# Image 0 of an attention layer: eight transposed runs in 96 steps for seven in 100, and the last group's column sums added on Pool

## The chip, the cores and the metric

The kernel runs on one core of a Trainium2 chip. The core has five engines that run at the same time and wait for each other by semaphores: PE (TensorE, matrix products), ACT (ScalarE, functions of one element, exp above all), DVE (VectorE), POOL (GpSimd) and SP (which here only issues DMAs). The trace lists PE's weight loads apart, as PEld. The metric is the device time of one execution in microseconds (us), as the median of several runs.

## The reference

The input is `x`, 4 images of 64 x 64 positions with 64 channels, float32. Four layers follow one another:

- layer 0: attention over the 4096 positions of an image, with query, key and value projections, times `gamma`, plus `x`
- layer 1: layer norm, a 1x1 convolution to 256 channels, a 3x3 depthwise convolution, a gate (product of the two halves), a scale by the channel means, a 1x1 convolution back, residual; then norm, 1x1, gate, 1x1, residual
- layer 2: attention of the image with itself, without weights
- layer 3: attention with projections to 32 channels, then a batch norm over all images, residual

The change lies in layer 2 of image 0:

```
def _L2_conv_ref(x):
    B, C, H, W = x.shape
    xf = x.reshape(B, C, H * W)
    scores = jnp.einsum('bci,bcj->bij', xf, xf)
    attn = jax.nn.softmax(scores, axis=-1)
    return jnp.einsum('bcj,bij->bci', xf, attn).reshape(x.shape) + x
```

`scores` is symmetric, 4096 x 4096 for each image: what is true of the pair (i, j) is true of (j, i).

## The kernel before

**Order of work.** The program is a list of items, one per step of an attention layer, that `run` (L1843) emits in order: layer 0 of images 0 to 3 (32 items each), layer 2 of image 0 (100 items), then layer 2 of image b and layer 3 of image b - 1 in turn. Each engine executes its own instructions in the order in which they are emitted. Beside the items run two lanes (`Lane`, L995): `conv` holds setup and layer 1, `misc` the projections, the features of layer 2 and the like. A lane is a generator that emits a piece of work and yields a price in microseconds; each item "ticks" the lane by some amount, and the lane emits its next piece when the ticks have paid for it. Layer 1 of image b starts two items after layer 0 of image b has ended, so layer 1 of image 3 runs beside layer 2 of image 0 and its tail beside layer 2 of image 1.

**Layer 2** (`layer2`, L1324). The 4096 columns and rows are cut into 8 groups of 512. A block (h, g) is exp(scores) for the columns of group h and the rows of group g. It takes two steps (u = 0, 1) of 256 rows. A step (`item`, L1495) does this:

- `score` (L1377): four matmuls (L1390, eight records in the trace) into a PSUM slot of 1024 columns, one of three that all work takes in turn; two exps on ACT (L1395) write half of an `e` tile and add up the rows. An `e` tile holds the two steps of a pair; the pool has six tiles, shared with `xr` (image 0's transposed weights), `esum` and `own`.
- `products` (L1445), two or three items later: four matmuls (L1451) add e times x into the accumulator of group h. When group h ends, ACT copies the accumulators to an `own` tile (L1463; image 0 only) and DVE adds that to `m.A` (L1466).

**Transposed runs.** Where the lists have a pair, such as `(1, 2)` in group 0, the blocks (0, 1) and (0, 2) also serve as (1, 0) and (2, 0), which are then not computed. For each of a pair's four steps DVE transposes e (`turned`, L1408), and a run of 64 matmuls (`turned_products`, L1468; L1477; 128 records) multiplies the transposed tiles with `xr`; DVE reads its two slots into `m.A` (L1490 or L1492). Image 0 issues a run three items after its last step, as long as an item of its layer 2 is left. The row sums of the mirrored blocks are column sums of e: `column_sums` (L1412). For image 0 Pool issues a DMA for each step (L1424) that copies or adds e to one of two halves of `esum`, and one at the group's end that adds the halves (L1428), and then adds the remaining two quarters (L1432); for the other images Pool itself adds e to `esum` (L1430, L1432). `spread_sums` (L1434), nine items after a group's last mirrored step, transposes and reduces `esum` on DVE; if the layer has ended by then, it comes at the sixth item of the next layer.

Image 0 uses the lists `PART`, images 1 to 3 `FULL` (L1317). Which groups of image 0 have pairs: 0, 1, 6 and 5, in this order of time; the order of groups is 0, 1, 2, 3, 4, 7, 6, 5.

**What stands around it.** In an item of image 0 the lane `conv` is ticked by 3.3, but by 1.5 in the seven items around the last step of the third run (`slow`, items 20 to 26), and `misc` by 1.8. Layer 1 of image 3 (L1199) uses them so: norm (L1159), whose factors SP spreads by DMA (L1183) and DVE multiplies in (L1191); 1x1 matmuls (L1205); two halves (r = 1, then r = 0) of 4 x 9 depthwise multiply-adds on DVE (L1240, L1243, L1251), each half beginning with ACT's writes to `pad` (L1222); `ytot`, the sum over positions (L1257); `sca`, the product for the scale (L1260); 1x1 (L1269); the second norm (L1170 to L1191); four pieces of 1x1, gate and 1x1 (L1205, L1290, L1294, L1297). From item 89 on, `features2(1)` (L1302) transposes image 1 on PE (L1309), in four pieces that DVE and then ACT copy (L1312) and SP spreads by DMA (L1313). `close2(0)` (L1529) scales and adds image 0's result in items 10, 13, 22, 32 and 42 of image 1; it first reduces the row sums, in one instruction for each run of groups with equal counts (L1540).

Of the kernel before, what the change touches and what calls it, by code (L numbers as in the profile page):

```python
# [691 lines left out]
def fast_path(ctx: ExitStack, tc: tile.TileContext, a: dict, out: bass.AP, bad):  # L692
# [43 lines left out]
    def piece():  # L736
        if turn_of["banks"]:
            return PS[:, bass.ts(new_bank(), 512)]
        return new_ps()[:, 0:512]
# [8 lines left out]
    def new_e(name="e"):  # L748
        return ep.tile([128, 2048], F32, tag="e", name=name)
# [4 lines left out]
    def new_big(name):  # L754
        return big.tile([128, 4096], F32, tag="big", name=name)
# [236 lines left out]
    def at(i, fn):  # L992
        due.setdefault(i, []).append(fn)
# [308 lines left out]
    def features2(b):  # L1302
        x = X[:, b]
        im[b].ko = ko = new_big("ko")
        kv = ko[:, 0:N].rearrange("p (a e n) -> p a e n", e=2, n=128)
        for g in range(4):
            ps = piece()
            for i in range(4):
                nc.tensor.transpose(ps[:, bass.ts(i, 128)], x[:, bass.ts(4 * g + i, 128)], ident)  # L1309
            for e, copy in enumerate((nc.vector.tensor_copy, nc.scalar.copy)):  # L1310
                own, other = slice(64 * e, 64 * e + 64), slice(64 - 64 * e, 128 - 64 * e)
                copy(kv[own, bass.ts(g, 4), e, :], ps[own, :].rearrange("p (a n) -> p a n", n=128))  # L1312
                nc.sync.dma_start(out=kv[other, bass.ts(g, 4), e, :], in_=kv[own, bass.ts(g, 4), e, :])  # L1313
            yield 3.0
# [1 line left out]
    SIDES = [[(7, (h + 1) % 7), ((h + 2) % 7, (h + 3) % 7)] for h in range(7)]  # L1316
    FULL = [(7, [7])] + [(h, [h] + SIDES[h]) for h in range(6)] + [(6, SIDES[6] + [6])]  # L1317
    PART = [
        (0, [0, 7, (1, 2), 5, (3, 4), 6]), (1, [1, 2, (5, 6), 3, 4, 7]), (2, [2, 1, 3, 4, 7]),
        (3, [3, 1, 2, 4, 7]), (4, [4, 1, 2, 3, 7]), (7, [7, 0, 1, 2, 3, 4]),  # L1320
        (6, [6, (2, 3), 0, (4, 7), 5]), (5, [5, (2, 3), 0, (4, 7), 6]),
    ]

    def layer2(b, when_free=None):  # L1324
# [87 lines left out]
        def column_sums(n):  # L1412
            h, _, _, run, _ = steps[n]
            if run is None:
                return
            k, e = mine_t[h].index(n), st["e"][n]
            if k == (0 if b == 0 else 1):
                st["esum"][h] = new_e("esum")
            if h not in st["esum"]:
                return  # L1420
            esum = st["esum"][h][:, 0:1024]
            if b == 0:
                both = st["esum"][h]
                nc.gpsimd.dma_start(  # L1424
                    out=both[:, bass.ts(k % 2, 1024)], in_=e, **({} if k < 2 else {"accum_op": ALU.add})
                )
                if n == mine_t[h][-1]:
                    nc.gpsimd.dma_start(out=esum, in_=both[:, 1024:2048], accum_op=ALU.add)  # L1428
            else:
                nc.gpsimd.tensor_add(esum, st["e"][mine_t[h][0]] if k == 1 else esum, e)  # L1430
            if n == mine_t[h][-1]:
                nc.gpsimd.tensor_add(esum[:, 0:512], esum[:, 0:512], esum[:, 512:1024])  # L1432
# [96 lines left out]
    def close2(b):  # L1529
        x, m = X[:, b], im[b]  # L1530
        ps, tot, n = piece(), sums2[:, b, :], 4 * max(m.mirrored) + 4
        cs = m.cs.rearrange("p (j k) -> p j k", k=4)
        for k in range(4):
            mm(ps[32 * k : 32 * k + 32, 0:n], sel4, cs[:, 0:n, k], start=True, stop=True)
        g = 0
        while g < 8:
            k = g
            while k < 8 and m.count[k] == m.count[g]:
                k += 1
            nc.vector.tensor_reduce(  # L1540
                tot[:, 4 * g : 4 * k],
                m.zs[:, m.first[g] : m.first[g] + 4 * m.count[g] * (k - g)]
                .rearrange("p (t k) -> p t k", k=m.count[g]), AX.X, ALU.add,
            )
            g = k
        nc.vector.tensor_add(tot[:, 0:n], ps[:, 0:n], tot[:, 0:n])
        rz = sm.tile([128, 32], F32, tag="rz2", name="rz2")
        nc.vector.reciprocal(rz, tot)
        yield
        for i in range(4):  # L1550
            ps = new_ps()
            for j in range(8):
                c = 1024 * i + 128 * j
                nc.tensor.transpose(ps[:, bass.ts(j, 128)], m.A[:, c : c + 128], ident)
            blocks_ = ps.rearrange("p (j n) -> p j n", n=128)
            nc.vector.tensor_mul(
                blocks_, blocks_, rz[:, bass.ts(i, 8)].unsqueeze(2).to_broadcast([128, 8, 128])
            )
            xs = x[:, bass.ts(i, 512)].rearrange("p (j h) -> p j h", h=H)
            for o in range(2):  # L1560
                nc.vector.tensor_add(xs, ps.rearrange("p (j o h) -> p j o h", j=8, o=2)[:, :, o, :], xs)  # L1561
            yield
# [9 lines left out]
    def open3(b):  # L1572
        x, m = X[:, b], im[b]
        m.tg = new_big("tg")
        m.th = m.tg[:, 0:1024]
        m.gx = m.tg[:, 1024:2048].rearrange("p (t d) -> p t d", d=32)
        for nb in range(2):
            ps = piece()
            for jj in range(2):
                for s in range(2):  # L1580
                    k = 2 * s + jj
                    mm(
                        ps[32 * k : 32 * k + 32, :], thw[64 * s : 64 * s + 64, :],
                        tok(x, s, 2 * nb + jj), start=True, stop=True,
                    )
            nc.vector.tensor_scalar_add(m.th[:, bass.ts(nb, 512)], ps, V("L3_conv_theta_b"))
            yield 3.0

        m.own = own = m.tg[:, 2048:3072].rearrange("p (s n) -> p s n", s=2)
        for s in range(2):  # L1590
            ps = piece()
            for j in range(4):
                mm(
                    ps[32 * j : 32 * j + 32, :], phw[64 * s : 64 * s + 64, :],
                    tok(x, s, j), start=True, stop=True,
                )
            nc.vector.tensor_scalar_add(own[:, s, :], ps, V("L3_conv_phi_b"))
            yield 3.0
        for i in range(2):
            ps = piece()  # L1600
            for t in range(8):
                mm(ps[:, bass.ts(t, 64)], x[:, bass.ts(8 * i + t, 128)], gw, start=True, stop=True)
            for s in range(2):
                nc.vector.tensor_add(
                    m.gx[:, 16 * s + 8 * i : 16 * s + 8 * i + 8, :],
                    ps.rearrange("p (t s d) -> p t s d", s=2, d=32)[:, :, s, :],
                    gb.unsqueeze(1).to_broadcast([128, 8, 32]),
                )
            yield 3.0

    def keys3(b):
        m = im[b]
        m.ph = new_big("ph")
        keys = m.ph.rearrange("p (s n) -> p s n", s=2)
        for j in range(4):
            for k in range(4):
                nc.sync.dma_start(
                    out=keys[32 * k : 32 * k + 32, :, bass.ts(j, 512)],
                    in_=m.own[32 * j : 32 * j + 32, :, :],
                )  # L1620
# [185 lines left out]
    conv_from, misc_from, misc_to = {}, {}, {}  # L1806
# [9 lines left out]
    for b in range(B):  # L1816
        misc_to[len(items)] = True
        f = len(items)
        if b == 0:
            layer2(b)  # L1820
            misc_from[f + 89] = [features2(b + 1)]
        else:
            layer2(b, lambda b=b: keys3(b - 1))
            turns = close2(b - 1)
            for i in (10, 13, 22, 32, 42) if b == 1 else (8, 12, 22, 32, 42):
                at(f + i, lambda turns=turns: next(turns))
            misc_from[f + 46] = [open3(b - 1)]
            f = len(items)
            misc_to[f] = True
            layer3(b - 1)  # L1830
            if b + 1 < B:
                turns = features2(b + 1)
                for i in (4, 7, 10, 13):
                    between3[f + i] = 2, lambda turns=turns: next(turns)
    f = len(items)
# [174 lines left out]
@with_exitstack  # L2010
def conv_seq_kernel(ctx: ExitStack, tc: tile.TileContext, a: dict, out: bass.AP):
    nc = tc.nc
    flag = ctx.enter_context(tc.tile_pool(name="flag", bufs=1))
    bad = flag.tile([1, 1], mybir.dt.int32, name="bad")
    fast_path(tc, a, out, bad)
    n_bad = nc.values_load(bad[0:1, 0:1], min_val=0, max_val=1 << 20)
    with tc.If(n_bad > 0):
        general_path(tc, a, out)
# [37 lines left out]
```

## Time and profile before

| | us |
|---|---|
| median of 3 runs | 2454.41 (2452.31 to 2454.88) |
| the profiled execution | 2454.17 |
| its span | 2452.4 |
| layer 2 of image 0, from the first product to the last | 1033 to 1249 |
| PE busy in that stretch of 216 us | 209.2 |
| ACT, DVE, Pool busy in it | 151.2, 155.3, 28.9 |
| mean share of the DMA engines in it | 0.47 |

Granted clock: 1.00 in all of these stretches. In the lists of instructions a line gives the start, the length, the engine, the source line, the operation, what it writes and reads, the shape and the number of records; in brackets the idle time of the engine before it and what ended that. Matmuls are pipelined: lengths overlap, and the time between two starts is what one costs. Waits on PE are found by these brackets; the page's share of busy time is a mean over stages with different limits.

### The profile page before, as it was taken

What the parts mean: (1) busy time and instruction counts of PE and PEld (TensorE: products, weight loads), DVE (VectorE), ACT (ScalarE), POOL (GpSimd) and SP (SyncE); (2) the same over time, 40 slices, a digit from 0 to 9 for tenths busy, and PEclk for the clock granted to TensorE, in tenths of its full rate; (3) what the DMA queues carried; (4) which work ended last, traced back from release to release, by engine and by line L of the source; (5) the groups of instructions that cost most, each with busy time, mean ns of one, the idle gap of its engine ahead of it and who ended that gap; (6) DMA issues with size and microseconds to landing.
All of it is one profiled execution on the core that took longest, in us unless ns stands there. A gap on an engine that the chain in (4) does not pass through costs nothing.

```text
span 2452.4 us, 63404 instructions
## 1 busy us (share of the span) xinstructions
PE 2412.2 (98%) x27381; PEld 930.4 (38%) x27381; DVE 1466.6 (60%) x1784; ACT 1651.8 (67%) x3146; POOL 531.7 (22%) x383
## 2 busy tenths in 40 slices
PE   9999999999999999999999999999999999999998
PEld 3343453336433643345334442144421344421113
DVE  2010377227722773378656668876668866678886
ACT  4666766666666676668664459954489744579996
POOL 2000000000000000010135561256631355622110
PEclk9999999999999999999999999999999999999999
DMA  3000000000000000150630026610075300386554
GB/s 80 1 18 1 19 1 18 18 19 1 18 18 11 8 18 18 48 127 2 136 72 20 20 66 134 140 25 24 15 155 117 74 21 20 74 168 142 118 118 116
DMA packets 67668, 136.39 MB, mean 56 GB/s; under 512 B 13004, under 2 KB 34229, under 8 KB 67381
## 3 DMA queue, kind: packets, MB, share of 16 engines
q0 software_dynamic: 24320, 86.55, 17.5%
q1 hardware_dynamic: 42309, 43.85, 7.8%
q8 instruction: 217, 3.56, 0.6%
q10 hardware_dynamic: 752, 1.85, 0.2%
q14 instruction: 70, 0.57, 0.1%
HBM read 4.80 MB, written 4.19 MB: 4 GB/s over the span
## 4 chain that ended last, share of the span: by engine, by line
PE 85%; DVE 9%; ACT 4%; issue 1%; SPq 1%; DMA 0%; DVEq 0%; ACTq 0%
PE PS L1121 18%; PE PS L1095 18%; PE PS L1390 9%; PE PS L1451 9%; PE PS L1639 8%; PE PS L1700 8%; PE PS L1477 7%; DVE tg L1691 3%; PE PS L1205 2%; ACT e L1650 2%; DVE y L1240 2%; DVE X L1561 1%; ACT e L1100 1%; PE PS L1170 1%; PE PS L1063 1%
## 5 line engine op out<-in xcount | busy, mean ns | idle before, releaser
L1100 ACT ACTIVATE e<-PS 128x1024 f32<-128x1024 f32 x512 | 524.2, 1024 | 332.2 <-PE PS L1095 299.6
L1395 ACT ACTIVATE e<-PS 128x512 f32<-128x512 f32 x632 | 371.5, 596 | 334.2 <-PE PS L1390 313.5
L1121 PE MATMUL PS<-e,vq 64*64 64x512 f32 x4096 | 577.1, 592 | 0.0
L1095 PE MATMUL PS<-X,q 64*64 64x512 f32 x4096 | 575.0, 591 | 1.8 <-DVE X L979 1.7
L1650 ACT ACTIVATE e<-PS 128x512 f32<-128x512 f32 (+2 forms) x588 | 500.2, 920 | 59.3 <-PE PS L1639 37.9
L1691 DVE TENSOR_TENSOR tg<-tg,e 128x2048 f32<-128x2048 f32 x172 | 393.8, 2290 | 42.8 <-ACT e L1650 30.8
L1390 PE MATMUL PS<-ko 64*64 64x512 f32 x2528 | 342.8, 596 | 1.1 <-ACT e L1395 0.6
L1451 PE MATMUL PS<-e,X 64*64 64x512 f32 x2528 | 335.6, 590 | 0.9 <-DVE X L1133 0.6
L1240 DVE SCALAR_TENSOR_TENSOR y<-pad,vec,y 128x1024 f32<-128x1024 f32 x240 | 309.1, 1288 | 15.9 <-ACT y L1236 8.5
L1430 POOL TENSOR_TENSOR esum<-esum,e 128x1024 f32<-128x1024 f32 x126 | 299.2, 2375 | 53.6 <-ACT e L1395 46.7
L1408 DVE STREAM_TRANSPOSE turned<-e 128x1024 f32<-128x1024 f32 x196 | 240.6, 1237 | 104.4 <-ACT e L1395 104.4
L1639 PE MATMUL PS<-tg,ph 32*64 32x512 f32 x4096 | 295.5, 612 | 1.7 <-ACT e L1650 0.8
L1095 PEld LDWEIGHTS PS<-X,q 64*64 64x64 f32 x4096 | 184.0, 133 | 258.9 <-issue 179.4
L1121 PEld LDWEIGHTS PS<-e,vq 64*64 64x64 f32 x4096 | 184.1, 133 | 252.0 <-issue 156.0
L1424 POOL DMA_DIRECT2D esum<-e x28 | 22.0, 787 | 1170.7 <-ACT e L1395 1158.9
L1700 PE MATMUL PS<-e,tg 128*32 128x512 f32 x2048 | 272.5, 604 | 0.0
L1108 DVE TENSOR_REDUCE sums<-zs 128x1 f32<-128x4 f32 x128 | 19.6, 153 | 260.4 <-ACT e L1100 260.2
L1451 PEld LDWEIGHTS PS<-e,X 64*64 64x64 f32 x2528 | 104.9, 133 | 168.1 <-issue 144.9
L1672 POOL DMA_DIRECT2D xn<-e x116 | 101.3, 906 | 292.4 <-ACT e L1650 205.0
L1390 PEld LDWEIGHTS PS<-ko 64*64 64x64 f32 x2528 | 97.9, 132 | 163.4 <-issue 136.6
L1639 PEld LDWEIGHTS PS<-tg,ph 32*64 32x64 f32 x4096 | 63.4, 129 | 223.4 <-ACT e L1650 191.0
L1395 ACT ACTIVATION_READ_ACCUMULATOR e<-PS 128x1 f32 x632 | 127.4, 202 | 0.0
(218 smaller groups left out, 1712.9 us busy)
## 6 DMA issues: line engine op xcount, KB each, us to landing
xn<-e POOLq DMA_DIRECT2D x132, 512.0 KB, 5.3
esum<-e POOLq DMA_DIRECT2D x28, 512.0 KB, 5.2
xn<-t SPq DMA_DIRECT2D x64, 128.0 KB
ph<-tg SPq DMA_DIRECT2D x64, 128.0 KB
xn<-X SPq DMA_DIRECT2D x224, 32.0 KB
xr<-X SPq DMA_DIRECT2D x176, 32.0 KB
ko<-ko SPq DMA_DIRECT2D x32, 128.0 KB
xr<-in_x_dram SPq DMA_DIRECT2D x13, 256.0 KB
```

The costliest lines, as they stand in the source:

```text
L1095: mm(ps[64 * c : 64 * c + 64, bass.ts(r, 512)], m.q[rows_, 128 * t + 64 * c : 128 * t + 64 * c + 64], x[rows_, bass.ts(g, 512)], start=Tru ...
L1100: act(es[g // 2][:, bass.ts(g % 2, 1024)], ps, AF.Exp, bias=SHIFT0, accum_out=zs[:, g : g + 1],)
L1121: ins = mm(PS[64 * s : 64 * s + 64, 2048 + 512 * j : 2560 + 512 * j], vq[rows_, :], es[j // 2][rows_, k : k + 512], start=t == 0 and i < 2 ...
L1240: stt(y1, win, wt, y1, ALU.mult, ALU.add)
L1390: mm(ps[64 * c : 64 * c + 64, bass.ts(r, 512)], m.ko[rows_, k : k + 64], m.ko[rows_, bass.ts(h, 512)], start=True, stop=True,)
L1395: act(e[:, bass.ts(r, 512)], ps[:, bass.ts(r, 512)], AF.Exp, bias=SHIFT2, accum_out=slot(g, 2 * u + r),)
L1430: nc.gpsimd.tensor_add(esum, st["e"][mine_t[h][0]] if k == 1 else esum, e)
L1451: mm(st["acc"][r][64 * c : 64 * c + 64, :], xw[rows_, 4 * g + 2 * u + c, :], st["e"][n][rows_, bass.ts(c, 512)], start=n == mine[h][0], st ...
L1639: mm(PS[64 * c : 64 * c + 64, bass.ts(banks[k], 512)], m.ph[32 * k : 32 * k + 32, 128 * mc + 64 * c : 128 * mc + 64 * c + 64], m.th[32 * k ...
L1650: act(e[:, 512 * lo : 512 * k], PS[:, 512 * banks[lo] : 512 * banks[lo] + 512 * (k - lo)], AF.Exp,)
L1691: nc.vector.tensor_add(esum, esum, e)
L1700: mm(st["y"][32 * k : 32 * k + 32, :], m.gx[:, i % 32, :], es[i][:, bass.ts(k, 512)], start=mc == 0, stop=i % 32 == 31,)
```

## The change

Three edits. The lists of image 0 are cut anew. Group 0 loses the direct block 5 and group 6 the direct block 5; group 5 has `(0, 6)` as a third pair where it had the direct blocks 0 and 6, and that pair stands for the two blocks that went. Together 96 steps for 100, and eight pairs for seven; the pairs of groups 6 and 5 now follow one another without direct steps between. `slow` is worked out from the third run and moves to items 18 to 24.

The column sums of group 5 in image 0 no longer go by DMA: Pool adds them, as it does for the other images, from the group's second mirrored step on.

The features of image 1 start at item 86 for 89.

```diff
     PART = [
-        (0, [0, 7, (1, 2), 5, (3, 4), 6]), (1, [1, 2, (5, 6), 3, 4, 7]), (2, [2, 1, 3, 4, 7]),
+        (0, [0, 7, (1, 2), 6, (3, 4)]), (1, [1, 2, (5, 6), 3, 4, 7]), (2, [2, 1, 3, 4, 7]),
         (3, [3, 1, 2, 4, 7]), (4, [4, 1, 2, 3, 7]), (7, [7, 0, 1, 2, 3, 4]),
-        (6, [6, (2, 3), 0, (4, 7), 5]), (5, [5, (2, 3), 0, (4, 7), 6]),
+        (6, [6, 0, (2, 3), (4, 7)]), (5, [5, (2, 3), (4, 7), (0, 6)]),
     ]
...
             k, e = mine_t[h].index(n), st["e"][n]
-            if k == (0 if b == 0 else 1):
+            moved = b == 0 and h != 5
+            if k == (0 if moved else 1):
                 st["esum"][h] = new_e("esum")
             if h not in st["esum"]:
                 return
             esum = st["esum"][h][:, 0:1024]
-            if b == 0:
+            if moved:
                 both = st["esum"][h]
                 nc.gpsimd.dma_start(
                     out=both[:, bass.ts(k % 2, 1024)], in_=e, **({} if k < 2 else {"accum_op": ALU.add})
                 )
...
         if b == 0:
             layer2(b)
-            misc_from[f + 89] = [features2(b + 1)]
+            misc_from[f + 86] = [features2(b + 1)]
```

## The prediction

> **What bounds the kernel now.** I read the page's totals and its chain first, then TensorE's order of time in layer 2 of image 0 (about 1033 to 1249 us), then who keeps TensorE waiting there.
>
> ```profile
> PE 2412.2 (98%) x27381; PEld 930.4 (38%) x27381; DVE 1466.6 (60%) x1784; ACT 1651.8 (67%) x3146; POOL 531.7 (22%) x383
> PE 85%; DVE 9%; ACT 4%; issue 1%; SPq 1%; DMA 0%; DVEq 0%; ACTq 0%
> ```
>
> TensorE is busy nearly all the span, and the chain lies on it for 85%. So TensorE work that goes is time that goes, unless TensorE then waits longer. The price of that work, from the order of time on PE (start, length):
>
> ```profile
> 1329.42 1.04 PE L1390 MATMUL PS<-ko 64*64 64x512 f32 x8
> 1330.28 1.04 PE L1451 MATMUL PS<-e,X 64*64 64x512 f32 x8
> 1331.25 3.71 PE L1477 MATMUL PS<-turned,xr 32*64 32x256 f32 x128
> 1334.89 1.09 PE L1390 MATMUL PS<-ko 64*64 64x512 f32 x8
> 1335.80 1.04 PE L1451 MATMUL PS<-e,X 64*64 64x512 f32 x8
> ```
>
> Neighbours overlap, so read from start to start. A score (L1390) takes 0.86 us, a product (L1451) 0.86: 1.72 a step. A turned run (L1477, 128 records) takes 3.64, and the groups beside it start 0.11 and 0.05 later than usual: 3.80.
>
> The waits that the change touches, on PE and then on DVE:
>
> ```profile
> 1181.34 0.35 PE L1260 MATMUL PS<-ytot,sca 128*128 128x1 f32 x2 [0.96 <-DVE ytot L1257]
> 1222.69 1.09 PE L1390 MATMUL PS<-ko 64*64 64x512 f32 x8 [0.15 <-ACT ko L1312]
> 1226.44 0.66 PE L1309 MATMUL PS<-ident,X 128*128 128x128 f32 x4 [0.94 <-ACT ko L1312]
> 1241.11 1.09 PE L1205 MATMUL PS<-xn,pw 64*64 64x512 f32 x8 [2.04 <-DVE xn L1191]
> 1280.64 1.09 PE L1205 MATMUL PS<-xn,pw 64*64 64x512 f32 x8 [0.66 <-DVE A L1492]
> ```
>
> ```profile
> 1181.03 0.16 DVE L1257 TENSOR_REDUCE ytot<-ysum 128x1 f32<-128x8 f32 x1
> 1181.11 0.68 DVE L1466 TENSOR_TENSOR A<-own,A 128x512 f32<-128x512 f32 x1
> 1238.70 1.25 DVE L1408 STREAM_TRANSPOSE turned<-e 128x1024 f32<-128x1024 f32 x1 [0.91 <-ACT e L1395]
> 1239.87 1.18 DVE L1191 TENSOR_TENSOR xn<-xn,X 128x1024 f32<-128x1024 f32 x1
> 1275.15 2.35 DVE L1297 TENSOR_TENSOR X<-X,t 128x512 f32<-128x512 f32 x1 [0.18 <-ACT t L1295]
> ```
>
> These PE waits come to 4.75 us. The last line is an add whose median is 0.69 us; it ran beside four Pool adds in a row (1269.71 to 1279.74).
>
> **The change part by part.** Items are numbered from the start of image 0's layer 2.
>
> *The lists.* 100 steps become 96: minus 4 x 1.72 = 6.88 us of TensorE. There are eight runs for seven, but a run is issued three items after its last step, and in both lists the last run ends too late for that (97 of 0 to 99; 95 of 0 to 95). The trace agrees: 6144 records of L1477 are 48 runs, 6 of image 0 and 42 of the others. So seven are issued for six: plus 3.80. Sum on TensorE: -3.08.
>
> Off the path: ACT loses 4 x 2 x (0.60 + 0.20) = 6.4 us; DVE gains four transposes (1.24 each) and four reads of a run (0.42 each), 6.6 us. From 1181 to 1249 ACT is busy 39.6 and DVE 36.6 of 68 us, and TensorE has that stretch covered; without that cover the 6.6 us would show whole. Close2 has six reduces for five: +0.18 us (L1540 rows) ahead of a scale that TensorE's next turned run can wait on.
>
> *Column sums of group 5.* Eight Pool DMA issues of 0.86 and the closing one go (nine transfers of 512 KB, landing after some 5.2); eleven adds of 2.37 come: 11 x 2.37 + 1.27 = 27.3 us on Pool. Cover: the twelve steps hold 12 x 1.72 plus three turned runs of 3.80 and four feature groups of 0.6, some 34 us of TensorE. Pool keeps up, and is ready for the first add at step 85: group 6's last add ended 12.7 us after its last DMA issue (1205.17 to 1217.89), and steps 82 to 85 with their run and convolution work take about as long. Spread_sums for group 5 comes five items into image 1, over 8 us after the last exp, against 3.7 for two Pool instructions. Queued behind Pool's adds is nothing until image 1's first sums. Cost 0; if the cover is gone, see the slower rival.
>
> *Group ends, two or four items earlier against image 3's layer 1.* The convolution lane is paid 3.3 an item, so its work keeps its item number up to 95, while groups 1 to 7 now end two items earlier. Group 7's add into A (L1466, 0.68) stood right behind ytot on DVE; its products end at item 69 now, so it stands ahead: ytot 0.6 later. From 1131.35 to 1181 DVE runs without a gap, so this reaches TensorE whole. Earlier, the slow stretch of the lane (items 20 to 26, now 18 to 24) leaves three more multiply-adds of 1.30 after the third run, and group 2's two adds (1.41) come before the half's end, against two more steps of time (3.44): +1.9, of which 1.07 is slack (1123.86 to the pad write at 1124.93). ACT's pad write, and with it the start of DVE's second half, is up to 0.8 later. I take 0.5, between 0 (ACT catches up) and 0.9. Together the 0.96 wait grows by 1.1 (0.6 to 1.5).
>
> *Multiply by the norm (L1191).* Its first half stays at item 95, now the last of the layer; its matmul follows in the next item, as before. It stands behind a transpose that waits for the exp. TensorE's work in between grows by two products, with which the layer closes (1.72), so the wait of 2.04 would fall to 0.3. But Pool now adds beside it, and two operands in SBUF cost L1297 1.66 us more. Three quarters of the time an add is running: I take +1.0, between 0 and 1.7. New wait 1.3, a gain of 0.7 (1.7 to 0).
>
> [...]
>
> *Features of image 1, items 86 to 90 (were 89 to 93).* Its eight SP transfers of 128 KB no longer run beside Pool's; SP's loads of xr keep their items (0, 10, 40, 50), at least 14 ahead of their runs. Each ACT copy stands behind a DVE copy, behind a transpose; all four meet a transpose (three before), but the adds from group 6's own copy are over earlier. Wait 1.1 before; I take 1.1, bounds 0 and 2.2.
>
> *Tail of image 3's layer 1.* It ends at item 18 of image 1, was 14. The wait of 0.66 recurs (item 10 has a matmul of L1205 in both), and two more pieces fall between runs: +0.2 with the reduce, bounds -0.3 and +1.0. Behind it the program is the same, and shifts.
>
> Sum: -3.08 + 1.1 - 0.7 + 0 + 0.2 = -2.5 us. The profiled execution took 2454.17 us (span 2452.4 and 1.8 around it), 0.24 under the median of 2454.41; so 2451.7 in a run like it, 2451.9 as a median. Bounds of the terms: -3.08 + 0.6 - 1.7 - 1.1 - 0.3 = -5.6, and -3.08 + 1.5 + 0 + 1.1 + 1.0 = +0.5.
>
> **Rivals.**
>
> *The waits go too.* If ytot is no later (ACT and DVE have slack I don't see), and the L1191 and feature waits vanish with the DMA traffic (busy share 0.73 to 0.94 in most of 1180 to 1250): -3.08 - 2.04 - 1.09 = -6.2, 2448.2. Against it: none of these waits is put down to a DMA.
>
> *The order is worse, the work less.* The tail in image 1, the feature copies and the e buffers (two sums held through items 18 to 22 and 85 to 90, of six) each cost their upper bound and one more exp wait of about 2 us: +0.5 + 2, 2456.9. For it: TensorE waited 1.81 for an exp at 1047. Against it: the layer has only some 7 us of PE waits in all.
>
> *Slower: group 6's transfers hold up Pool.* They are eight in a row now. At 9.6 us (the longest landing) for 5.2, four in a chain, the last lands 17.6 us later; Pool's adds may start about 9 late before pairs are held and TensorE waits: 17.6 - 9 - 3.1, +5.5, 2459.9. It decides from a lateness over 9 us. Against it: the median is 5.2 with the same neighbours.
>
> *The change saves nothing*, if TensorE waits for DVE anyway: 0, 2454.4. DVE was gapless only up to 1181; the removed steps lie after it.
>
> **How the numbers follow.** 0.2% is 4.9 us, about what a measurement can tell from no change. Forecast 0.54; waits go too 0.21; order worse 0.12; slower 0.08; nothing saved 0.05. Faster: the second case (0.20 of it) and a little of the first, 0.22. Slower: the fourth and a third of the third, 0.12. Same: 0.66. The forecast's own range is 2448.8 to 2454.9. Wanted are 8 in 10: from the second case to just short of the slower one, 2448.0 to 2457.0.
>
> **What would show it.** Right: 896 records of L1477 in image 0; 96 steps; 11 adds of 2.37 in group 5 with Pool idle between; L1260 waiting about 2 us; L1191 longer than 1.18 or its wait under 2; image 1 shifted by 2 to 3 us with the rest unchanged. Wrong: a wait on Pool ahead of L1395 or L1390, exps waiting for e buffers, a PE wait over 3 us in items 74 to 95, or a changed image 1 after item 20.

## The result: 0.13% slower

The changed kernel takes 2457.61 us (median; 2456.23 to 2462.32), the kernel before 2454.57 beside it. The ratio is 1.0013, with a 95% interval of 1.0007 to 1.0019. The forecast was 2451.9 with a range up to 2457.0: the time lies above the range. The changed kernel's profiled execution took 2457.62 us; its span of 2455.5 is 3.1 longer than the one before.

The totals and the chain of the changed kernel's page:

```profile
PE 2410.4 (98%) x27445; PEld 918.3 (37%) x27445; DVE 1473.2 (60%) x1793; ACT 1645.6 (67%) x3130; POOL 551.5 (22%) x385
PE 83%; DVE 9%; ACT 4%; issue 1%; DMA 1%; SPq 1%; POOL 0%; DVEq 0%; ACTq 0%; POOLq 0%
```

TensorE has 64 records more than before, as worked out (four steps of 16 less, one run of 128 more), and is busy 1.8 us less. The work shrank and the span grew, so TensorE waits longer. POOL and POOLq are new in the chain. Who keeps TensorE waiting in layer 2 of image 0 (line, releaser, its line: us in all, times, longest):

```profile
PE PS L1390 <- DVE A L1493: 5.5, 2, 5.2
PE PS L1205 <- DVE xn L1191: 1.5, 1, 1.5
PE PS L1205 <- ACT e L1395: 1.2, 1, 1.2
PE PS L1309 <- ACT ko L1312: 0.9, 1, 0.9
PE PS L1478 <- ACT ko L1312: 0.9, 1, 0.9
...
PE PS L1260 <- DVE ytot L1257: 0.4, 1, 0.4
```

The first line has no counterpart before. L1493 is DVE's copy of a transposed run from PSUM (lines from 1418 on have moved by one). Here it is in DVE's order of time, around the third run, which ended on TensorE at 1086.2:

```profile
1081.62 0.71 DVE L1441 STREAM_TRANSPOSE esum<-esum 128x512 f32<-128x512 f32 x1
1091.95 0.69 DVE L1442 TENSOR_REDUCE cs<-esum 128x16 f32<-128x512 f32 x1 [9.63 <-POOL cs L1439]
1092.56 1.41 DVE L1493 COPY A<-PS 128x256 f32<-128x256 f32 x4
```

In the kernel before the same reduction waits for nobody:

```profile
1085.09 0.69 DVE L1441 TENSOR_REDUCE cs<-esum 128x16 f32<-128x512 f32 x1
```

In the changed kernel DVE stands still for 9.63 us at the reduction of group 0's column sums, because Pool has not yet zeroed `cs`, the tile that it writes. Pool's order of time says why:

```profile
1080.38 0.90 POOL L1425 DMA_DIRECT2D esum<-e  x1 [2.51 <-DMA esum<-e]
1085.57 0.87 POOL L1429 DMA_DIRECT2D esum<-esum  x1 [4.29 <-DMA esum<-e]
1090.51 1.25 POOL L1433 TENSOR_TENSOR esum<-esum 128x512 f32<-128x512 f32 x1 [4.08 <-DMA esum<-esum]
1091.72 0.19 POOL L1439 MEMSET cs<- 128x128 f32 x1
```

The same in the kernel before:

```profile
1082.39 0.88 POOL L1424 DMA_DIRECT2D esum<-e  x1 [2.27 <-ACT e L1395]
1082.96 0.53 POOL L1438 MEMSET cs<- 128x128 f32 x1
1084.16 0.88 POOL L1424 DMA_DIRECT2D esum<-e  x1 [0.68 <-ACT e L1395]
1090.23 0.86 POOL L1428 DMA_DIRECT2D esum<-esum  x1 [5.18 <-DMA esum<-e]
1095.27 1.27 POOL L1432 TENSOR_TENSOR esum<-esum 128x512 f32<-128x512 f32 x1 [4.18 <-DMA esum<-esum]
```

The memset of 0.19 us stands in `spread_sums(0)`, which comes at item 22 in both kernels (group 0's last mirrored step is item 13 in both). Group 1's mirrored steps, however, moved from items 20 to 23 up to items 18 to 21. So the memset was emitted among group 1's four transfers before, and is emitted behind the whole group now: behind the closing transfer, which waits until the four have landed, and behind the closing add, which waits until the closing transfer has landed. Behind DVE's reduction stand the PSUM reads of the third run; until they are done TensorE has no slot to score into:

```profile
1087.09 1.04 PE L1452 MATMUL PS<-e,X 64*64 64x512 f32 x8
1093.36 1.98 PE L1390 MATMUL PS<-ko 64*64 64x512 f32 x8 [5.23 <-DVE A L1493]
1095.12 1.93 PE L1452 MATMUL PS<-e,X 64*64 64x512 f32 x8
1096.82 1.93 PE L1390 MATMUL PS<-ko 64*64 64x512 f32 x8
1098.53 1.26 PE L1452 MATMUL PS<-e,X 64*64 64x512 f32 x8
```

After the wait of 5.23 us the groups stand 1.76, 1.70, 1.71 and 1.09 apart, not 0.86 to 0.91: 2.77 us more. The windows show the reason (busy us of each engine, then the granted clock, PEclk, then the DMA share and GB/s):

```profile
1080.00:1088.00 8.00, 8.00 (x172) 4.00 (x162) 2.33 (x4) 4.23 (x12) 1.76 (x2) 1.00 0.70 136
1088.00:1093.40 5.40, 0.17 (x8) 0.05 (x4) 1.45 (x4) 0.58 (x3) 1.40 (x2) 0.89 0.54 114
1093.40:1096.00 2.60, 2.60 (x16) 0.77 (x20) 2.56 (x4) 0.56 (x2) 0.00 (x0) 0.50 0.20 51
1096.00:1099.00 3.00, 3.00 (x20) 0.94 (x16) 2.93 (x3) 0.90 (x5) 0.00 (x0) 0.50 0.13 33
1099.00:1102.00 3.00, 3.00 (x32) 1.00 (x28) 2.89 (x4) 2.31 (x8) 0.00 (x0) 1.00 0.02 5
```

The clock is halved for some 6.8 us (5.6 in two windows, 1.2 in the window at 0.89). The wait and the half clock together cost 5.23 + 2.77 = 8.0 us.

The account nearly closes. From the first exp of layer 2 (1019.49 before, 1018.50 after) to one and the same exp of image 1 (the read of its row sum, at 1401.12; 1404.64) the changed kernel takes 386.14 us for 381.63: +4.51. Of that -3.08 is TensorE's work, +8.0 this stall, and the other listed waits are 0.7 shorter (8.0 for 8.7), which makes +4.2; 0.3 us are left over. Ahead of it that execution was 0.99 shorter and behind it 0.4, where the change alters nothing: 4.51 - 0.99 - 0.4 = 3.1, the difference of the spans.

### The profile page after: what moved, and what is told of

Same layout as the page of the kernel before. It is cut to its first block, busy times and chain, and to the rows that moved or that the text cites. A ratio compares the mean times of both kernels' runs of the same rounds, so it can differ in the third digit from the quotient of the medians.

```text
span 2455.5 us, 63512 instructions
## 1 busy us (share of the span) xinstructions
PE 2410.4 (98%) x27445; PEld 918.3 (37%) x27445; DVE 1473.2 (60%) x1793; ACT 1645.6 (67%) x3130; POOL 551.5 (22%) x385
## 4 chain that ended last, share of the span: by engine, by line
PE 83%; DVE 9%; ACT 4%; issue 1%; DMA 1%; SPq 1%; POOL 0%; DVEq 0%; ACTq 0%; POOLq 0%
PE PS L1121 18%; PE PS L1095 18%; PE PS L1390 8%; PE PS L1640 8%; PE PS L1452 8%; PE PS L1701 8%; PE PS L1478 7%; DVE tg L1692 3%; PE PS L1205 2%; DVE y L1240 2%; ACT e L1651 2%; ACT e L1395 1%; DVE turned L1408 1%; DVE X L1562 1%; ACT e L1100 1%
## 5 line engine op out<-in xcount | busy, mean ns | idle before, releaser
L1395 ACT ACTIVATE e<-PS 128x512 f32<-128x512 f32 x624 | 366.2, 595 | 342.3 <-PE PS L1390 319.8
L1390 PE MATMUL PS<-ko 64*64 64x512 f32 x2496 | 336.1, 599 | 6.2 <-DVE A L1493 5.5
L1431 POOL TENSOR_TENSOR esum<-esum,e 128x1024 f32<-128x1024 f32 x136 | 323.2, 2377 | 59.5 <-ACT e L1395 52.0
L1452 PE MATMUL PS<-e,X 64*64 64x512 f32 x2496 | 327.5, 592 | 1.4 <-ACT own L1464 0.8
L1408 DVE STREAM_TRANSPOSE turned<-e 128x1024 f32<-128x1024 f32 x200 | 245.8, 1238 | 107.0 <-ACT e L1395 107.0
L1425 POOL DMA_DIRECT2D esum<-e x20 | 15.6, 782 | 1151.5 <-ACT e L1395 1031.1
L1452 PEld LDWEIGHTS PS<-e,X 64*64 64x64 f32 x2496 | 97.8, 133 | 172.9 <-issue 152.5
L1390 PEld LDWEIGHTS PS<-ko 64*64 64x64 f32 x2496 | 89.9, 133 | 173.7 <-issue 143.8
```

Source lines behind the costliest of these rows:

```text
L1390: mm(ps[64 * c : 64 * c + 64, bass.ts(r, 512)], m.ko[rows_, k : k + 64], m.ko[rows_, bass.ts(h, 512)], start=True, stop=True,)
L1395: act(e[:, bass.ts(r, 512)], ps[:, bass.ts(r, 512)], AF.Exp, bias=SHIFT2, accum_out=slot(g, 2 * u + r),)
L1452: mm(st["acc"][r][64 * c : 64 * c + 64, :], xw[rows_, 4 * g + 2 * u + c, :], st["e"][n][rows_, bass.ts(c, 512)], start=n == mine[h][0], st ...
```

## The experiments

Kernels with added lines have their numbers shifted by up to three: L1390, L1442 and L1478 of the changed kernel are L1393, L1444 and L1480 in most.

**Theory and rivals.** W: the memset's place in Pool's queue costs some 8 us, and the rest of the change gains what was forecast. Rivals: D, that it is DVE's wait as such, with the multiply-adds that it delays, which costs; and that the new lists are worse in themselves.

**cs_zeroed_early**: the changed kernel, with `cs` zeroed at the first score of the layer.

```diff
+                if b == 0:
+                    m.cs = sm.tile([128, 128], F32, tag="cs2", name="cs2", bufs=1)
+                    nc.gpsimd.memset(m.cs, 0.0)
...
-                m.cs = sm.tile([128, 128], F32, tag="cs2", name="cs2", bufs=1)
-                if b == 0:
-                    nc.gpsimd.memset(m.cs, 0.0)
+                if b:
+                    m.cs = sm.tile([128, 128], F32, tag="cs2", name="cs2", bufs=1)
```

> The changed kernel, but the zeroing of cs (a Pool memset of 0.19 us) is emitted at item 0 of image 0's layer 2, not at item 22, where in the changed kernel it stands on Pool behind the closing transfer and the closing add of group 1. Theory W (the wait): this memset holds DVE for 9.6 us, DVE's reads of the third run hold TensorE for 5.2, and TensorE's clock at 0.50 afterwards costs 2.8 more. All 8.0 go: about 2449.6 us (2448 to 2451.5), under the kernel before, with no DVE wait on POOL and clock 1.00 from 1088 to 1100. Rival D (DVE is late anyway: the moved slow stretch and group ends put more on DVE there): the wait moves to ytot, under 3 us gained, 2454.5 to 2456.5. Rival P (Pool's eleven adds or the closer runs cost the time): as the changed kernel, 2457.6 within 1.

Measured: 2451.83 us (2450.02 to 2455.80), ratio to before 0.9993 [0.9984, 1.0002]. DVE's order of time now:

```profile
1083.07 0.69 DVE L1444 TENSOR_REDUCE cs<-esum 128x16 f32<-128x512 f32 x1
1087.18 1.42 DVE L1495 COPY A<-PS 128x256 f32<-128x256 f32 x4 [3.42 <-PE PS L1480]
```

The reduction waits for nobody, the PSUM reads wait for the run alone, TensorE has no wait there, and the clock is 1.00 from 1080 to 1106. That is 5.8 us off the median (4.9 by the ratios, since the two kernels were measured in different rounds) and 7.35 off the stretch between the two exps (378.79). The difference between these numbers lies at least in part at item 10, whose wait varies between executions, of which more below. The median is 0.3 above the range expected of this run. It is 2.35 us under the kernel before beside it (2454.18), with an interval that just includes no change. That it meets the forecast's 2451.9 to 0.1 us is partly luck: seven executions lie at 2450.0 to 2452.0 and four at 2454.7 to 2455.8.

**before_spread_late**: the kernel before, with the memset moved behind group 1's closing add by coming two items later.

```diff
-        spread_at = {mine_t[h][-1] + (5 if b else 9): h for h in m.mirrored}
+        spread_at = {mine_t[h][-1] + (5 if b else 11 if h == 0 else 9): h for h in m.mirrored}
```

> The kernel before, with one edit: the spreading of group 0's sums, and the memset in it, moves from item 22 to item 24, so that the memset stands behind group 1's closing transfer and add, as in the changed kernel. The lists, the DMA sums and the features are untouched. Theory W: DVE waits until about 1097 for the memset, TensorE for some 5 us behind the third run, then half clock: 5 to 9 us more, 2460 to 2463.5. Rivals D and P, to which the lists or Pool's adds matter: 0 to 2 us more.

Measured: 2461.35 us (2459.94 to 2463.31), ratio 1.0031 [1.0019, 1.0043]: the stall can be made in the kernel before, without one step of the change. Its memset stands at 1094.90, right behind the closing add (1093.69). DVE, and TensorE:

```profile
1095.13 0.69 DVE L1441 TENSOR_REDUCE cs<-esum 128x16 f32<-128x512 f32 x1 [8.90 <-POOL cs L1438]
```

```profile
1097.73 1.98 PE L1390 MATMUL PS<-ko 64*64 64x512 f32 x8 [5.90 <-DVE A L1492]
```

**before_spread_late_cs_early** is its control: the same late sums, with `cs` zeroed early by the edit shown above.

> Control of the run before it in this list: the kernel before, spreading of group 0 at item 24 as there, but the memset at item 0. Theory W: the place of the spreading itself costs nothing, as the kernel before within 1 us (2453.6 to 2455.6). If moving DVE's two instructions by two items were what costs, it would be as slow as the run before it.

Measured: 2454.14 us, ratio 1.0004 [0.9995, 1.0013]. Two items more or less for the sums themselves are free; the two kernels differ in the memset's place alone, and are 7.2 us apart.

**cs_zeroed_between**: the changed kernel, with the memset between group 1's closing transfer and its closing add.

```diff
                     nc.gpsimd.dma_start(out=esum, in_=both[:, 1024:2048], accum_op=ALU.add)
+                    if h == 1:
+                        m.cs = sm.tile([128, 128], F32, tag="cs2", name="cs2", bufs=1)
+                        nc.gpsimd.memset(m.cs, 0.0)
```

> The changed kernel, but the memset stands on Pool between group 1's closing transfer and its closing add: DVE still waits for it, but until about 1086.7 and not 1091.9, before the third run has ended (1086.2) by little. Theory W: what costs is TensorE's wait and the clock after it, not DVE's; DVE's wait of some 4 us stays and the time is within 1 us of the run with the memset at item 0, 2449.5 to 2451.5. Rival D (each microsecond DVE loses here is paid at ytot): about 4 us slower than that run, 2453 to 2455.

Measured: 2452.67 us (2450.15 to 2455.79), ratio 0.9992 [0.9983, 1.0001]. DVE still waits here, and TensorE does not:

```profile
1091.08 0.69 DVE L1444 TENSOR_REDUCE cs<-esum 128x16 f32<-128x512 f32 x1 [3.98 <-POOL cs L1432]
```

A wait of 3.98 us on DVE costs nothing, one of 9.63 costs 8: it counts from where the third run's reads become due. The median is over the range that was expected (2449.5 to 2451.5) and close to D's 2453, so it doesn't decide; the trace does. TensorE has no wait at the third run, and its wait for `ytot`, where D would be paid, is 1.03 us, for 1.02 in cs_zeroed_early. What makes the profiled execution long is a wait at item 10 (below). D falls.

With the cause found, four kernels went after the rest of the change, each with `cs` zeroed early and one edit more. They are compared with cs_zeroed_early, which was measured in an earlier round (the kernel before took 2454.18 us beside it, 2453.75 beside these four). Each ratio is known to some 2.2 us, so differences of medians of 1 to 2 us are not clear of noise by themselves; the stretch between the two exps and the waits in the profiles carry these readings, one execution each.

**cs_early_dma_sums** (`moved = b == 0`): group 5's sums by DMA again.

> cs_zeroed_early with the column sums of group 5 back on the DMAs, as before the change. By my theory (the changed kernel lost its time to the memset alone; Pool's adds cost TensorE about nothing, because the multiply L1191, stretched from 1.18 to 2.41 us beside an add, has the last two products of the layer ahead of its matmul): the multiply is back at about 1.18, the wait of L1205 on it goes from 1.5 to between 0.3 and 2, and the time stays within 1.5 us of cs_zeroed_early's 2451.8. Rival (Pool's adds hold DVE up and this is paid by TensorE): the wait falls by the whole 1.2 us and the time to about 2450.5. Rival (the transfers collide with the features of image 1): the wait of L1309 grows from 0.9 to 2 or more, time 2453 or above.

Measured: 2455.56 us (2453.04 to 2458.27), ratio 1.0005 [0.9996, 1.0014]. The third expectation has the time and the collision, but the wrong place: L1309 still waits 0.94. The multiply L1191 is back at 1.18 us and TensorE's wait for it is gone, but the first score of image 1 waits for its features:

```profile
1251.45 1.09 PE L1393 MATMUL PS<-ko 64*64 64x512 f32 x8 [2.33 <-DMA ko<-ko]
```

From the last run to the common exp the profiled execution takes 2.24 us more than cs_zeroed_early: 2.33 for this wait, less 1.54 for the multiply, and about 1.1 of gaps among the layer's last products (24 records in 3.89 us, for 2.76 usually). The whole stretch between the exps is 5.4 longer (384.18); the other 3.1 is a stall at item 10 (a wait of 2.17 for 0.64, and 1.7 lost at half clock), to which I come below. How the 3.7 us between the medians divide isn't shown.

**cs_early_features_late** (`f + 89` for `f + 86`): the features three items later, Pool's adds kept.

> cs_zeroed_early with the features of image 1 at item 89 again instead of 86. My theory, on record as 0 with bounds 0 and 2.2 of waits: the two feature waits together (1.9 us in the changed kernel's profile) become about 1 as in the kernel before, the time falls by 0 to 1 us, to 2451 to 2452. Rival (the earlier start is needed because the layer has four items fewer, so that image 1's first scores wait for their features): a wait of TensorE at L1390 on ACT's or a DMA's features in the first items of image 1, 2 us or more, time 2453.5 or above.

Measured: 2450.27 us (2449.15 to 2453.62), ratio 0.9986 [0.9977, 0.9995]. Both feature waits (0.94 each) are gone, and no score of image 1 waits. The stretch between the exps is 1.46 shorter (377.33): the earlier start costs 1.5 us here and buys nothing. I had expected 0 to 1.

**cs_early_dma_sums_features_late**: both edits together.

> cs_early_dma_sums (group 5's sums by DMA, memset early) with the features at item 89 instead of 86. cs_early_dma_sums showed what I had not priced: TensorE waited 2.3 us at image 1's first score for the DMA that spreads its features, which ran beside group 5's sums. Theory (sums and features share the DMA engines, so the one part of the change needs the other): started three items later the features land later still, the wait of L1393 on a DMA grows from 2.3 to 5 us or more, time 2458 or above. Rival (the wait has nothing to do with the order of the transfers): it stays at 1.5 to 3, time 2453.5 to 2456.

Measured: 2458.54 us (2455.20 to 2462.31), ratio 1.0020 [1.0011, 1.0029].

```profile
1252.26 1.98 PE L1393 MATMUL PS<-ko 64*64 64x512 f32 x8 [7.87 <-DMA ko<-ko]
```

So the sums' transfers and the features share the DMA engines (their mean share is 0.83 from 1250 to 1254 here), and the new lists, four items shorter, have no time for both. Either Pool adds the sums, or the features start early and still come 2.3 us late. With Pool's adds the start at item 86 is not needed.

**cs_early_slow_20_26** (`slow = range(20, 27)`): the slow stretch of the lane as it was before.

> cs_zeroed_early with the slow stretch of the lane at items 20 to 26 as in the kernel before, instead of 18 to 24. My forecast put 0.5 us (0 to 0.9) of the wait of L1260 down to the earlier slow stretch. If that holds, L1260 waits about 0.5 us instead of 1.0 and the time is 2451.3. Rival (the wait stems from group 7's add alone, or varies by itself): L1260 stays at 0.7 to 1.3. Risk: the third run's DVE reads then meet more multiply-adds, TensorE waits 1 to 2 us there, time 2453.

Measured: 2449.56 us (2448.68 to 2454.27), ratio 0.9981 [0.9972, 0.9990]. L1260 waits 0.40 us for 1.02, the wait for `own` at group ends falls by 0.3, and the stretch between the two exps is 1.33 us shorter (377.46). That is more than the 0.5 that I had expected. The median fell by 1 us more than this; only one of these executions is above 2452, for five of cs_zeroed_early's, and item 10 may be all of that, but it isn't shown.

**cs_early_pool_0_and_5** (`moved = b == 0 and h not in (0, 5)`): group 0's sums by Pool as well. At item 10 a matmul of layer 1 (L1205) waits for DVE's multiply by the norm's factors, which SP spreads by eight transfers, while group 0's eight transfers of 512 KB run; the DMA share there is 0.93 to 1.04.

> cs_zeroed_early with the column sums of group 0 also added by Pool instead of by DMA. In the profiles the wait of L1205 on the multiply of item 10, which stands behind a DMA of the norm's factors, is 0.64 to 3.3 us from one execution to the next; group 0's eight transfers of 512 KB run just before it. If they are its cause, the wait stays near 0.6, the spread of the runs (2450.0 to 2455.8) narrows to its lower end and the median is about 2450.5. [...] Third: the wait comes from something else and nothing moves, 2451.8.

Measured: 2449.62 us (2449.06 to 2451.24), ratio 0.9981 [0.9972, 0.9990]: no wait at item 10, a spread of 2.2 us for 5.8, and 0.62 less between the exps (378.17).

**before_pool_0**: the same edit in the kernel before (`moved = b == 0 and h != 0`).

> The kernel before, with one edit: the sums of group 0 added by Pool instead of by DMA. Theory (group 0's transfers delay the norm's factors at item 10, TensorE waits 0.6 to 3.3 us there, and some executions lose 1.7 us more by 3.4 us at half clock): L1205 waits at most 0.3 at item 10, the runs lose their upper cluster at item 10, the median goes from 2454 to about 2452 (2451 to 2452.8). Rival (the better executions of cs_early_pool_0_and_5 had another cause): median unchanged, 2453.5 to 2454.8.

Measured: 2451.12 us (2450.23 to 2452.64), ratio 0.9991 [0.9982, 1.0001]; the kernel before beside it 2453.4 (2451.52 to 2457.24). The interval just reaches no change. The multiply and the matmul behind it in the kernel before, and the two multiplies in this one:

```profile
1046.26 1.23 DVE L1191 TENSOR_TENSOR xn<-xn,X 128x1024 f32<-128x1024 f32 x1 [5.63 <-DMA xn<-t]
1047.59 1.21 PE L1205 MATMUL PS<-xn,pw 64*64 64x512 f32 x8 [1.81 <-ACT e L1395]
```

```profile
1040.44 2.28 DVE L1191 TENSOR_TENSOR xn<-xn,X 128x1024 f32<-128x1024 f32 x1
1048.05 2.40 DVE L1191 TENSOR_TENSOR xn<-xn,X 128x1024 f32<-128x1024 f32 x1
```

The matmul's wait is listed under ACT's exp, but it starts 0.1 us after the multiply ends (1046.26 + 1.23 = 1047.49). Beside Pool's adds the multiply takes a microsecond more, but it starts 5.6 earlier, counted from the layer's first exp, and is waited for by nobody. The wait that goes is 1.8 us in the profile of before, and in other executions it costs more: in that of cs_zeroed_between, where L1205 waited 3.34 us, the clock was halved afterwards.

```profile
1047.00:1050.00 3.00, 0.91 (x9) 0.68 (x13) 2.24 (x2) 0.06 (x1) 0.86 (x1) 1.00 0.98 194
1050.00:1053.00 3.00, 3.00 (x28) 1.09 (x28) 1.37 (x2) 1.38 (x2) 0.00 (x0) 0.50 0.60 116
1053.00:1056.00 3.00, 3.00 (x112) 2.35 (x104) 0.00 (x0) 0.00 (x0) 0.00 (x0) 0.93 0.02 5
```

That is 3.4 us at half clock, 1.7 us lost on top. The profiled execution of cs_early_dma_sums shows the same after a wait of 2.17. In cs_early_pool_0_and_5 and before_pool_0, which don't have this wait, the spread is 2.2 and 2.4 us, for 5.8 and 5.7 with it: this place makes most of it there.

**combined**: memset early, slow stretch at 20 to 26, features at 89, groups 0 and 5 on Pool.

> The changed kernel with four things together: memset early, slow stretch at items 20 to 26, features at item 89, group 0's sums also by Pool. If the four effects seen alone stand beside each other, against cs_early_pool_0_and_5 (2449.6, few runs above it) the wait of L1260 goes from 1.0 to 0.4 and the two feature waits (1.9) go: 2447.2, between 2446.5 and 2448.5, and no runs at 2454. Rival (the gains of the four were one and the same, runs without the half clock at item 10): 2449 to 2450.

Measured: 2447.26 us (2446.74 to 2448.51), ratio 0.9972 [0.9961, 0.9983]. It beats both kernels: 0.28% under the one before, 10.35 us under the changed one's median (10.1 by the ratios). The four effects stand nearly side by side: the stretch between the exps is 375.74 us, 3.05 less than cs_zeroed_early's, for 1.33 + 1.46 + 0.62 of the three edits alone. What TensorE still waits for:

```profile
PE PS L1205 <- DVE xn L1191: 1.5, 1, 1.5
PE PS L1454 <- ACT own L1466: 0.8, 1, 0.8
PE PS L1393 <- ACT e L1398: 0.6, 1, 0.6
```

**combined_all_but_6** (`moved = b == 0 and h == 6`): group 1 on Pool too.

> As combined, with group 1's sums also added by Pool, so that only group 6's go by DMA. The four adds of 2.37 us stand beside DVE's multiply-adds of layer 1, of which some have two operands in SBUF. Theory: TensorE has those covered, the time is that of combined within 1 us. Rival: DVE falls behind in the first half of the convolution, the wait of L1260 grows to 2 or more, time 2449 to 2451.

Measured: 2453.05 us (2452.15 to 2455.11), ratio 0.9997 [0.9988, 1.0006], 5.8 slower than combined. The theory missed, and the rival had the wrong place. DVE, and TensorE:

```profile
1077.42 5.50 DVE L1243 SCALAR_TENSOR_TENSOR yg<-pad,vec,y 128x512 f32<-128x512 f32 x2
1082.84 2.36 DVE L1411 STREAM_TRANSPOSE turned<-e 128x1024 f32<-128x1024 f32 x2
```

```profile
1085.25 5.40 PE L1480 MATMUL PS<-turned,xr 32*64 32x256 f32 x128 [3.84 <-DVE turned L1411]
```

Two multiply-adds that take 1.42 us together in combined take 5.50 beside two Pool adds (1076.37 to 1082.36), 4.08 more; the third run's last transposes stand behind them, TensorE waits 3.84 and runs 3.4 us at half clock. So both sides were longer beside each other: the multiply-adds by 4.08 us, the two adds by 1.25 (5.99 for 2 x 2.37). How they hold each other up isn't shown.

## Why the prediction was wrong

**The step that failed** is "Group ends, two or four items earlier". It followed the earlier group ends on DVE and ACT and left out Pool, where each group also issues a closing transfer that waits for the group's landings and a closing add that waits for that transfer. The only thing said of what stands behind another in Pool's queue was "Queued behind Pool's adds is nothing until image 1's first sums", and that spoke of group 5. Nothing was said of what is queued behind group 1's closing transfer. One instruction was: the memset of `cs`, bound to group 0's item count. It was to be had from the profile of before: the memset at 1082.96 among the transfers (0.6 us behind an issue, 1.2 ahead of the next), the closing transfer at 1090.23 and the add at 1095.27, waiting 5.18 and 4.18 us. Group 1 two items earlier, memset where it was, is enough to see the order turn over; DVE's 9.6 and TensorE's 5.2 follow from the 0.19 us instruction's new place. The half clock then adds 2.8, and nothing in the profile of before showed one in this layer.

**TensorE -3.08: right.** 27445 records for 27381; with the memset out of the way the stretch between the exps is 2.84 shorter than before.

**L1260, +1.1: the size roughly, the place not.** Group 7's add does stand ahead of `ytot` now (0.69 us, at 1180.94 ahead of 1181.55 in cs_zeroed_early). But L1260 itself waits 1.02 us there for 0.96 (0.40 in the changed kernel), and the wait for `own` at group ends, which I had not priced, takes 1.1 in all for 0.3. Of the two together, +0.9, the slow stretch's new place accounts for more than the 0.5 that I took: moving it back takes away 0.62 and 0.3 of waits, and 1.33 us in all.

**L1191, -0.7: right in sign and kind.** Its first half takes 2.41 us for 1.18 beside a Pool add (+1.23; I took 1.0), and the wait went from 2.04 to 1.55. The 1.0 came from one row, L1297's 2.35 us beside four Pool adds for a median of 0.69. The transposes beside the same adds took 1.23 to 1.25 (the median of all 196 is 1.245); why the one is longer there and the others aren't, no run shows.

```profile
1251.69 2.41 DVE L1191 TENSOR_TENSOR xn<-xn,X 128x1024 f32<-128x1024 f32 x1
```

**Features, 0: +0.8,** inside the bounds (0.94 twice, for 0.94 and 0.15). **The tail, +0.2:** -0.4 (waits of 0.28, 0.30, 0.32 for 0.66, 0.29, 0.32). In cs_zeroed_early the smaller terms come to 0.9 - 0.5 + 0.8 - 0.4 = +0.8, for +0.6 in the forecast. That they agree is partly luck, since the parts don't; and with item 10's wait 1.2 shorter in that execution (0.64 for 1.81), which the change doesn't touch, the stretch should have fallen by some 3.4, not 2.84. The 0.6 stay open.

**Pool's adds, 0: right for the kernel that was forecast,** since Pool keeps up: group 6's closing add ends at 1220.2 and group 5's first add starts there, and Pool idles 0.8 to 2.4 us ahead of four of the later ones. But 0 hides that with the sums on DMA the shorter layer would have cost 2 us more at its end, and 7.87 of waiting with the features at item 89. The parts of the change are not independent, and I costed them as if they were.

**The rivals.** "Slower: group 6's transfers hold up Pool" had the right sign and the right engine, and the wrong group: group 6 delays nobody. "The waits go too" and "the order is worse" are not what happened: with the memset aside the layer is neither. The wait of 1.81 that spoke for the second was not for an exp, as I read it, but for the multiply of item 10. The chance of 0.08 for Pool as a source of delay was too small for a queue of which I had followed only one end.

## What to carry to other kernels

Where steps are moved against each other, list for every in-order queue what now stands behind an instruction that waits, the small ones too: a memset of 0.19 us, emitted two steps' worth later in its queue, cost 8 us. Zero a tile where its engine waits for nobody. When a transfer goes to an engine or back, look at who else uses the DMA engines at that time (beside the sums' transfers the features kept TensorE waiting for 2.33 or 7.87 us), and which DVE instructions are longer beside that engine's adds (here L1191 with 2.41 us for 1.18, and two multiply-adds with 5.50 for 1.42): the same edit gained 2.3 us in group 0 and lost 5.8 in group 1.

## What I had not expected of the hardware

In these executions a wait of TensorE could cost more than its length, and not only a long one. Half clock followed waits of 3.34, 3.84, 5.23, 5.90 and 7.87 us: for 3.4 us with the first, the second and the fourth, for 6.8 with the third, and for at least 6.2 with the last (clock 0.50 from 1250 to 1254 and 0.73 from 1254 to 1258 in cs_early_dma_sums_features_late). It also followed one of 2.17 (cs_early_dma_sums), and in before_spread_late one of 2.04 at L1191. The same wait of 2.04 in the profile of before was followed by full clock (1.00 from 1238 to 1250), and so were one of 1.81 there (1.00 from 1047 to 1053) and one of 2.33 in cs_early_dma_sums (the next two groups start 0.89 and 0.85 us apart). The profiled executions of before_spread_late_cs_early and before_pool_0 have this wait of 2.0 at L1191 too, and a mean clock of 0.999, as that of before has. The windows of before_spread_late around its wait of 2.04:

```profile
1244.00:1246.00 2.00, 1.02 (x12) 0.14 (x4) 1.34 (x2) 1.50 (x6) 0.86 (x1) 1.00 0.06 16
1246.00:1248.00 2.00, 0.94 (x8) 0.43 (x12) 2.00 (x2) 0.39 (x2) 0.87 (x1) 0.83 0.93 178
1248.00:1250.00 2.00, 2.00 (x14) 0.57 (x12) 1.27 (x2) 1.08 (x1) 0.00 (x0) 0.50 0.98 182
1250.00:1252.00 2.00, 2.00 (x20) 0.73 (x16) 0.00 (x0) 0.42 (x2) 0.00 (x0) 0.82 0.87 164
```

Counted from the end of the wait, half clock lasted 5.6, 2.8 and 3.9 us after the waits of 5.23, 5.90 and 7.87, where it had begun before the wait ended, and about 3.4 after the other four. So here a wait of 2.04 or 2.17 us could be followed by half clock, and one of 2.33 was not; what decides between them isn't shown. My estimate from these profiles, in which it followed two of six waits of 2.0 to 2.33 us: such a wait carries one chance in three of 1.7 us more, and to take it away gains more than its length.
